# A first attention unit's queues, and the start of the second layer: who loads, subtracts and copies, and in which order

## The chip, the cores and the metric

The kernel runs on one core of one Trainium2 chip. The metric is the device time of one execution in microseconds (us), from the first to the last instruction and what lies around them. TensorE (PE) multiplies matrices, ScalarE (ACT) and VectorE (DVE) work element by element, GpSimd (POOL) does so too and issues DMAs, and SyncE (SP) issues DMAs only. Each engine has one queue, worked in order; engines wait for each other on semaphores.

## The reference

Two layers over x of shape (2, 128, 64, 64), seen as two images of 4096 positions with 128 channels.

```python
# layer 0: group norm, then attention with four heads of 32 channels
qkv = jnp.einsum('oc,bcl->bol', w_qkv, xi) + b_qkv[None, :, None]
q, k, v = jnp.split(jnp.transpose(qkv, (0, 2, 1)), 3, axis=2)
q = _apply_rotary(pos, q)          # t * cos + (t with neighbours swapped and signed) * sin
k = _apply_rotary(pos, k)
...
weight = jnp.einsum('bct,bcs->bts', qh * scale, kh * scale)
weight = jax.nn.softmax(weight.astype(jnp.float16), axis=-1).astype(weight.dtype)
a = jnp.einsum('bts,bcs->bct', weight, vh).reshape(b, c, L)
hout = jnp.einsum('oc,bcl->bol', w_proj, a) + b_proj[None, :, None]
...
# layer 1: layer norm, then attention of the tokens with themselves
scores = jnp.einsum('bsd,btd->bst', x, x)
attn_weights = jax.nn.softmax(scores, axis=-1)
return jnp.einsum('bst,btd->bsd', attn_weights, x)
...
# and then a spectral unit: causal convolutions with 16 filters by FFT, 2 x 16 matrices,
# chosen among four branches by weights from log_weights and gumbel
```

## The kernel before

**Layer 0** runs in four units: image b and pair of heads pr. A unit first prepares its operands in eight blocks of 512 positions (i, in pairs i2), and then, for each of its two heads, multiplies scores (s), takes exponentials on ACT (e, line 443) and weighs the values with them (acc). While one unit is in its scores, the next is prepared beside it. Only the first unit, `first` in the code, has nothing to hide behind: its preparation and its own first scores run together, from about 27 to 86 us.

One block of the preparation: TensorE multiplies (`first`), VectorE adds the bias and multiplies by the rotary tables `tab` (line 236, twice), adds both halves (line 240), and takes the largest value (line 243). The result t is split into two float16 terms, the first being t rounded (`hi`, on ACT in the first unit) and the second the rest t - hi (`lo`, line 242). The values are split into three bfloat16 terms: `left` is the sum with the bias (line 270), a cast makes a term (line 273), and a difference takes it off what is left (line 275), so three casts and two differences a block. In the first unit the casts are ACT's and the differences GpSimd's.

After each pair of blocks, `stacks` (lines 277 to 286) copies the terms by DMA into the stacks ks and qs, of four strips of 32 rows each: ks takes first, first, second, second; qs takes first, second, first, second. That is 16 DMAs a pair. In the first unit SyncE issues the eight of ks and four of qs, GpSimd four of qs. SyncE also issues the tables (line 224): two wait in buffers, the next is loaded when one has been used, and its place in SyncE's order is behind the stacks of the pair before.

The last step of a head is `divide`: three parts of accs are added to ao, the row of sums is brought over by DMA (rec), inverted, sent to memory and brought back (back), and multiplied in (line 355). A `wait` count says how many turns to let pass before the last product; it is 5 for the last head of layer 0, 1 for all others.

**The joint.** The second layer needs its tokens as fp32r in a first part (hi, hiT) and a second (lo, loT). The second parts were written to memory (lows) beside layer 0 and are loaded again one at a time into `low`, one buffer, and copied to loT and lo (lines 1092, 1093). Before them stands the load of fw (line 796), in space that the last unit's operands still hold. The scores of layer 1 (y, line 911) are three products of these parts; their exponentials (ey) are split again (ep, lines 968 and 969), and their transposes too (eT, lines 929 and 930).

Beside attention of the first image (`attend(0)`), a chain of steps is interleaved: the second image's layer norm, `filters` (tb, lines 812 to 818), and `matrices`. The latter begins with `branch_weights` (z, zm, soft, zs, sm, top, free, wbr; lines 830 to 851) and the 16 coef (line 872), then mu, and then makes 16 matrices pm, each a weighted sum of four (lines 726 and 728) and two differences (lines 890 and 891), from `raw` loaded two matrices ahead. The buffer of the first raw is that of mu_raw and of tb.

What sets the order: a planner places every instruction on its engine's queue by estimated times, so a change at one place can move instructions elsewhere. An instruction that is given to `tc.keep_in_program_order` comes after everything that its engine was given before it in the program; all products of `product` are pinned so. The code at the joint:

```python
fw = transform(p1)                      # line 1082
...
def ready(i):                           # called by attend(0) as block i begins
    for n in range(2) if i == 0 else [i + 1]:
        if n < NQ:
            low = p.tile([P, 2, 512], F32, tag="low", name=f"low{n}")
            nc.sync.dma_start(low, lows[n].rearrange("n p c -> p n c"))
            nc.vector.tensor_copy(loT[0][:, bass.ts(n, 512)], low[:, 0])
            nc.vector.tensor_copy(lo[0][:, bass.ts(n, 512)], low[:, 1])
```

Of the kernel before, what the change touches and what calls it, by code (L numbers as in the profile page):

```python
# [12 lines left out]
F32 = mybir.dt.float32  # L13
# [6 lines left out]
ALU = mybir.AluOpType  # L20
AX = mybir.AxisListType

P = 128
# [5 lines left out]
NQ = L // 512  # L29
# [34 lines left out]
def conv_attn_hybrid(ctx: ExitStack, tc: tile.TileContext, io):  # L64
    nc = tc.nc
# [25 lines left out]
    def pool(stack, name, bufs=1, **kw):  # L91
        return stack.enter_context(tc.tile_pool(name=name, bufs=bufs, reuse_waits="tile", **kw))
# [82 lines left out]
    def layer0(tok, px, last, side, beside_last):  # L175
# [3 lines left out]
        with ExitStack() as l0:  # L179
            p1 = pool(l0, "l0_1")  # L180
# [26 lines left out]
            def prepare(b, pr, xn):  # L207
# [9 lines left out]
                first = (b, pr) == (0, 0)  # L217
# [46 lines left out]
                def split(at, n, pv):  # L264

                    bvb = bv[:, 2 * CH * pr : 2 * CH * pr + 2 * CH].rearrange("p (g c) -> p g c", g=2)

                    pool_, tag = (p1, f"ao{at // n % 3}") if first else (p2, "left")
                    left = pool_.tile([P, n, 2, CH], F32, tag=tag, name=f"left{u}_{at}", bufs=1)
                    nc.vector.tensor_tensor(left, pv, bvb.unsqueeze(1).to_broadcast([P, n, 2, CH]), ALU.add)  # L270
                    for k in range(NV):
                        dst = v[:, at : at + n, :, CH * k : CH * k + CH]
                        (nc.scalar.copy if first else nc.vector.tensor_copy)(dst, left)
                        if k + 1 < NV:
                            (nc.gpsimd if first else nc.vector).tensor_tensor(left, left, dst, ALU.subtract)

                def stacks(i2, term):
                    for s, stack in ((1, ks), (0, qs)):
                        for g in range(2):
                            for r in range(4):  # L280
                                src = term[r // 2 if s else r % 2]
                                at = 64 * s + CH * g
                                (nc.sync if first and (s or r >= 2) else nc.gpsimd).dma_start(
                                    stack[CH * r : CH * r + CH, g, bass.ts(i2, 1024)],
                                    src[at : at + CH, :],
                                )
# [48 lines left out]
            def divide(b, h, c, accs, wait):  # L335

                u = f"{b}_{h}_{c}"
                if h == 0:  # L340
                    ao[b, c] = (last if c == 3 else p1).tile([P, 1024], F32, tag=f"ao{c}", name=f"ao{b}_{c}", bufs=1)
                own = ao[b, c][CH * h : CH * h + CH, :]
                parts = [accs[CH * n : CH * n + CH, :] for n in range(NV)]
                rec = last.tile([CH, 1024 // CH], F32, tag="rec", name=f"rec{u}")
                nc.sync.dma_start(rec, accs[NV * CH :, :].rearrange("o (r s) -> o r s", r=CH))
                nc.vector.tensor_tensor(own, parts[0], parts[1], ALU.add)
                yield
                nc.vector.tensor_tensor(own, own, parts[2], ALU.add)
                nc.vector.reciprocal(rec, rec)
                back = dram.tile([CH, 1024 // CH], F32, tag="rec", name=f"back{u}", bufs=4)  # L350
                nc.sync.dma_start(back, rec)
                nc.sync.dma_start(parts[0], back.rearrange("r s -> (r s)").partition_broadcast(CH))
                for _ in range(wait):
                    yield
                nc.vector.tensor_tensor(own, own, parts[0], ALU.mult)
                yield
# [47 lines left out]
            for n, (b, pr) in enumerate(units):  # L404
# [16 lines left out]
                for g, i, m in order:  # L421
# [20 lines left out]
                    own = slice(0, len(tiles))  # L442
# [291 lines left out]
    def layers(st, layer0):  # L734
# [10 lines left out]
        hi, lo, hiT, loT = [], [], [], []  # L745
        lows = dram.tile([NQ, 2, P, 512], F32, name="lows")
# [36 lines left out]
        left = layer0(tok, px, last, side, beside_last)  # L783
# [9 lines left out]
        def transform(p):  # L793

            fw = p.tile([P, 4, NF], F32, name="fw", bufs=1)
            nc.sync.dma_start(fw, io["fw"])
            return fw
# [24 lines left out]
        def branch_weights(p):  # L822

            lg = p.tile([P, 2, NBR], F32, name="lg")
            nc.gpsimd.dma_start(lg[:, 0, :], io["log_weights"].partition_broadcast(P))
            nc.gpsimd.dma_start(lg[:, 1, :], io["gumbel"].partition_broadcast(P))
            z = p.tile([P, NBR], F32, name="z")
            nc.vector.tensor_tensor(z, lg[:, 0, :], lg[:, 1, :], ALU.add)  # L830
            zm = p.tile([P, 1], F32, name="zm")
            nc.vector.tensor_reduce(zm, z, AX.X, ALU.max, negate=True)
            zs = p.tile([P, 1], F32, name="zs")
            soft = p.tile([P, NBR], F32, name="soft")
            nc.scalar.activation(soft, z, AF.Exp, bias=zm, accum_out=zs)
            nc.vector.reciprocal(zs, zs)
            nc.vector.tensor_scalar(soft, soft, zs, None, ALU.mult)
            sm = p.tile([P, 1], F32, name="sm")
            nc.vector.reduce_max(sm, soft, axis=AX.X)
            top = p.tile([P, NBR], F32, name="top")  # L840
            nc.vector.tensor_scalar(top, soft, sm, None, ALU.is_equal)
            free = p.tile([P, NBR], F32, name="free")
            nc.vector.memset(free, 1.0)
            for i in range(1, NBR):
                nc.vector.scalar_tensor_tensor(
                    free[:, i : i + 1], top[:, i - 1 : i], 0.0, free[:, i - 1 : i], ALU.is_equal, ALU.mult
                )
            nc.vector.tensor_tensor(top, top, free, ALU.mult)
            wbr = p.tile([P, NBR], F32, name="wbr")
            nc.vector.tensor_tensor(wbr, top, soft, ALU.subtract)  # L850
            nc.vector.tensor_tensor(wbr, wbr, soft, ALU.add)
            ends = p.tile([P, NBR, P], F32, tag="phi", name="ends")
            nc.gpsimd.dma_start(ends, io["ends"].partition_broadcast(P))
            weighted_sum(mask, ends, top)
            return wbr
# [223 lines left out]
        with ExitStack() as l1:  # L1079
            p1 = pool(l1, "l1")  # L1080
            lo.append(p1.tile([P, L], F32R, name="lo"))
            fw = transform(p1)
            with ExitStack() as part:
                p = pool(part, "l1_a")
                gate = [0]

                def ready(i):
                    for n in range(2) if i == 0 else [i + 1]:
                        if n < NQ:
                            low = p.tile([P, 2, 512], F32, tag="low", name=f"low{n}")  # L1090
                            nc.sync.dma_start(low, lows[n].rearrange("n p c -> p n c"))
                            nc.vector.tensor_copy(loT[0][:, bass.ts(n, 512)], low[:, 0])
                            nc.vector.tensor_copy(lo[0][:, bass.ts(n, 512)], low[:, 1])

                def closed(j):
                    gate[0] = j + 1

                y = [None]

                def stage(i, n):  # L1100
                    y[0] = p.tile([P, 512], F32, tag="y", name=f"y1_{i}")
                    return y[0]

                stats = LayerStats(p1, tok[1], "a1")
                steps = chain(left, stats.steps(), filters(p, fw), matrices(p), normalise(1, stats, stage, gate))
                attend(0, p1, steps, closed, ready)
            right0.close()

            mxr, mxl = (x[0].rearrange("p (k s c) -> p k s c", k=NK, s=2) for x in (hiT, loT))
            with ExitStack() as part:  # L1110
                p = pool(part, "l1_b", 2)
                fed = LayerStats(ffw, tok[1], "f1")

                def closed(j):
                    fed.take(range(4 * j, 4 * j + 4))
                    fed.close(range(4 * j, 4 * j + 4))
                    own = slice(2 * j, 2 * j + 2)
                    m = p.tile([P, 2, 2, C], F32, tag="m", name=f"m{j}")
                    nc.sync.dma_start(m, mx[own].rearrange("k p s c -> p k s c"))
                    nc.vector.tensor_copy(mxr[:, own], m)  # L1120
                    nc.vector.tensor_tensor(mxl[:, own], m, mxr[:, own], ALU.subtract)

                attend(1, p1, feed(0, p, bank, fw), closed)
# [172 lines left out]
        fw = transform(late_pool)  # L1296
# [155 lines left out]
```

## Time and profile before

| what | us |
|---|---|
| median of 3 runs | 2924.3 (2923.4 to 2927.8) |
| the profiled execution | 2924.8 |
| its span | 2923.0 |
| TensorE, VectorE, ACT, GpSimd busy | 2852.4, 1689.9, 1916.1, 653.8 |
| first exponential of the first unit | starts at 45.48 |
| last accs copy of layer 0 ends | 1028.24 |
| first use of loT by TensorE | 1033.04 |
| pm loop on VectorE | 1118.6 to 1198 |

The page gives shares over the whole span. The two places that the change touches are some 60 and some 170 us of 2923, so their waits are read from the list of waits of each engine and from the timeline. In a timeline line, the text in brackets is the idle time of the engine just before the instruction, and what ended it. SPq lines are DMA issues of SyncE: the time is that of the issue, not of the transfer. The mean granted TensorE clock of this execution was 0.993 of full speed.

### The profile page before, as it was taken

The page shows a single profiled execution, that of the slowest core. Times are in us where ns is not written, and L with a number is a line of the kernel's source. Part 1 is how long each engine was busy: PE and PEld are TensorE (multiplying, and loading weights), DVE is VectorE, ACT ScalarE, POOL GpSimd, SP SyncE. Part 2 cuts the span into 40 slices and gives each one's busy share as a digit, 9 for nine tenths or more (in the row PEclk, how much of TensorE's full clock was granted, in tenths as well). Part 3 has the DMA queues.
Part 4 walks back from the last instruction along what each step waited for, and adds up shares of the span by engine and source line. Part 5 has one row for each costly group of instructions (what it writes and reads, how often), then busy time and mean ns, then how long its engine had stood idle before and what let it go on. Part 6 is the DMA issues. An engine that isn't in the chain of part 4 may idle for free. (4 is left out here: it accounts for less than half of the span.)

```text
span 2923.0 us, 40062 instructions
## 1 busy us (share of the span) xinstructions
PE 2852.4 (98%) x13872; PEld 1815.1 (62%) x13872; DVE 1689.9 (58%) x2916; ACT 1916.1 (66%) x2507; POOL 653.8 (22%) x1312
## 2 busy tenths in 40 slices
PE   5999999999999999999999999999999999999998
PEld 3555555555455577787777885666666666666665
DVE  5265562355243289877866677555555555555554
ACT  4999999999999956565555664444444444444442
POOL 3022120022000010000102003343444444444440
PEclk9999999999999999999999999999999999999999
DMA  4122120021001024100011002333333334333331
GB/s 137 33 63 77 48 66 16 5 78 48 6 33 35 4 83 128 57 1 1 26 39 40 8 26 68 97 89 93 92 85 82 81 77 115 82 85 84 82 82 54
DMA packets 166033, 175.91 MB, mean 60 GB/s; under 512 B 45264, under 2 KB 109536, under 8 KB 165824
## 3 DMA queue, kind: packets, MB, share of 16 engines
q1 hardware_dynamic: 122528, 137.05, 16.9%
q0 software_dynamic: 40304, 32.99, 5.4%
q10 hardware_dynamic: 2992, 3.22, 0.3%
q8 instruction: 115, 1.88, 0.3%
q14 instruction: 94, 0.77, 0.1%
HBM read 130.68 MB, written 25.49 MB: 53 GB/s over the span
## 5 line engine op out<-in xcount | busy, mean ns | idle before, releaser
L443 ACT ACTIVATE e<-s 128x1536 f16<-128x1536 f32 (+1 forms) x704 | 937.4, 1427 | 34.8 <-PE s L190 29.6
L1196 DVE TENSOR_TENSOR xl<-cv,xh 128x1024 fp32r<-128x1024 f32 x512 | 603.2, 1220 | 436.3 <-ACT xh L1195 349.0
L1195 ACT CAST xh<-cv 128x1024 fp32r<-128x1024 f32 x512 | 494.6, 1018 | 522.7 <-PE cv L1186 511.8
L1161 POOL DMA_DIRECT2D tokens_in<-rows x1024 | 490.5, 487 | 680.0 <-PE cv L1186 580.7
L190 PE MATMUL s<-qs,ks 128*128 128x512 f16 x2048 | 557.7, 379 | 11.8 <-ACT e L443 7.4
L190 PE MATMUL acc<-e,v 128*97 128x512 f16 x2048 | 557.1, 379 | 3.3 <-DVE accs L391 0.2
L1218 PE MATMUL m<-xh,loT 128*128 128x512 f32 x1024 | 409.5, 400 | 0.0
L1218 PE MATMUL m<-xh,hiT 128*128 128x512 f32 x1024 | 403.0, 394 | 0.0
L190 PEld LDWEIGHTS <-v 128*97 128x97 bf16 x2048 | 254.5, 124 | 214.3 <-issue 11.8
L190 PEld LDWEIGHTS <-ks 128*128 128x128 f16 x2048 | 200.5, 99 | 232.6 <-issue 46.9
L920 ACT ACTIVATE ey<-y,nshift 128x512 f32<-128x512 f32 x288 | 195.9, 689 | 201.4 <-PE y L911 179.2
L1186 PE MATMUL cv<-tables_in,tokens_in 32*128 32x512 f32 x2048 | 300.3, 646 | 1.8 <-DVE xl L1196 1.8
L1218 PE MATMUL m<-xl,hiT 128*128 128x512 f32 x1024 | 291.8, 417 | 1.2 <-DVE xl L1196 0.5
L1218 PEld LDWEIGHTS m<-xl,hiT 128*128 128x128 f32 x1024 | 178.6, 189 | 175.7 <-issue 104.7
L1218 PEld LDWEIGHTS m<-xh,loT 128*128 128x128 f32 x1024 | 192.5, 188 | 90.7 <-issue 47.8
L1218 PEld LDWEIGHTS m<-xh,hiT 128*128 128x128 f32 x1024 | 192.3, 188 | 42.2
L930 DVE TENSOR_TENSOR eT<-eT,eT 128x512 fp32r<-128x512 f32 x224 | 147.3, 684 | 112.9 <-ACT eT L929 112.0
L937 PE MATMUL oacc<-ep,hi 128*128 128x512 f32 x576 | 209.1, 411 | 1.2 <-DVE ep L969 1.2
L969 DVE TENSOR_TENSOR ep<-ey,ep 128x512 fp32r<-128x512 f32 x288 | 191.3, 684 | 7.6 <-PE oacc L937 1.4
L391 DVE COPY accs<-acc 97x512 f32<-97x512 f32 x64 | 44.2, 691 | 253.3 <-PE acc L190 253.3
L929 ACT ACTIVATE eT<-eT 128x512 fp32r<-128x512 f32 x224 | 133.1, 605 | 55.7 <-PE eT L927 55.5
L937 PE MATMUL oacc<-eT,hi 128*128 128x512 f32 x448 | 154.1, 405 | 2.2 <-DVE oT L975 1.2
(197 smaller groups left out, 3031.3 us busy)
## 6 DMA issues: line engine op xcount, KB each, us to landing
tables_in<-tables SPq DMA_DIRECT2D x1024, 64.0 KB, 3.3
tab<-in_rot SPq DMA_DIRECT2D x32, 512.0 KB, 4.1
tokens_in<-rows POOLq DMA_DIRECT2D x1024, 16.0 KB, 3.2
rows<-uh SPq DMA_DIRECT2D x64, 128.0 KB, 1.9
qs<-term POOLq DMA_DIRECT2D x112, 64.0 KB, 2.0
ks<-term POOLq DMA_DIRECT2D x96, 64.0 KB, 1.9
accs<-back SPq DMA_DIRECT2D x32, 128.0 KB, 2.3
lows<-stage SPq DMA_DIRECT2D x16, 256.0 KB, 2.0
```

What stands on the lines that cost most here:

```text
L190: tc.keep_in_program_order(nc.tensor.matmul(*args, **kw))
L443: nc.scalar.activation(e[:, own, :], ps[:, own, :], AF.Exp, scale=SCORE_SCALE)
L920: nc.scalar.activation(e[:, 2 * h + q, :], ps[:, q, :], AF.Exp, bias=nshift, accum_out=den[:, t, i : i + 1])
L929: nc.scalar.activation(eT[0], pt, AF.Copy, accum_out=den[:, 4 * i + u, j : j + 1])
L930: nc.vector.tensor_tensor(eT[1], pt, eT[0], ALU.subtract)
L937: nc.tensor.matmul(acc, a[0][:, own], c, start=(start and t == 0 and n == 0), stop=(stop and t == len(es) - 1 and n == 2),)
L969: nc.vector.tensor_tensor(es[t][1], e[:, t, :], es[t][0], ALU.subtract)
L1161: nc.gpsimd.dma_start(ut[part, :, :], rows[b][ci, row : row + BP, w0 : w0 + WC // 2, :])
L1186: nc.tensor.matmul(pu[:, h, :], ut[grp, w % 2, :], tt[grp, w % 2, :], start=True, stop=True)
L1195: nc.scalar.copy(hi, pu.rearrange("d h (c k) -> d k h c", k=NK))
L1196: nc.vector.tensor_tensor(seconds[n % 2][:, :, w, 64 * g2 : 64 * g2 + 64].rearrange("d k (h c) -> d k h c", h=2), pu.rearrange("d h (c k) ...
L1218: nc.tensor.matmul(acc, m, x, start=(s == 0 and w == 0 and i == 0), stop=(s == 1 and w == WC - 1 and i == len(products) - 1),)
```

## The change

Four things. In the first unit the value differences go from GpSimd to VectorE. Its stacks are shared out by term: SyncE issues those of the first terms (4 of ks and 4 of qs a pair), GpSimd those of the second. In `divide`, for the last head alone, the first addition is pinned behind what VectorE was given before it. At the joint, the first low load and its copies stand ahead of fw in the program, the copy to loT is pinned, later loads come one at a time, and the first instruction of the branch weights is pinned.

```diff
                         if k + 1 < NV:
-                            (nc.gpsimd if first else nc.vector).tensor_tensor(left, left, dst, ALU.subtract)
+                            nc.vector.tensor_tensor(left, left, dst, ALU.subtract)
...
                             for r in range(4):
-                                src = term[r // 2 if s else r % 2]
+                                n = r // 2 if s else r % 2
+                                src = term[n]
                                 at = 64 * s + CH * g
-                                (nc.sync if first and (s or r >= 2) else nc.gpsimd).dma_start(
+                                (nc.sync if first and n == 0 else nc.gpsimd).dma_start(
...
-                nc.vector.tensor_tensor(own, parts[0], parts[1], ALU.add)
+                terms = nc.vector.tensor_tensor(own, parts[0], parts[1], ALU.add)
+                if wait > 1:
+                    tc.keep_in_program_order(terms)
...
-            nc.vector.tensor_tensor(z, lg[:, 0, :], lg[:, 1, :], ALU.add)
+            tc.keep_in_program_order(nc.vector.tensor_tensor(z, lg[:, 0, :], lg[:, 1, :], ALU.add))
...
-            fw = transform(p1)
             with ExitStack() as part:
                 p = pool(part, "l1_a")
                 gate = [0]
 
+                def second_parts(n):
+                    if n < NQ:
+                        low = p.tile([P, 2, 512], F32, tag="low", name=f"low{n}")
+                        nc.sync.dma_start(low, lows[n].rearrange("n p c -> p n c"))
+                        copy = nc.vector.tensor_copy(loT[0][:, bass.ts(n, 512)], low[:, 0])
+                        if n == 0:
+                            tc.keep_in_program_order(copy)
+                        nc.vector.tensor_copy(lo[0][:, bass.ts(n, 512)], low[:, 1])
+
                 def ready(i):
-                    for n in range(2) if i == 0 else [i + 1]:
-                        if n < NQ:
-                            low = p.tile([P, 2, 512], F32, tag="low", name=f"low{n}")
-                            nc.sync.dma_start(low, lows[n].rearrange("n p c -> p n c"))
-                            nc.vector.tensor_copy(loT[0][:, bass.ts(n, 512)], low[:, 0])
-                            nc.vector.tensor_copy(lo[0][:, bass.ts(n, 512)], low[:, 1])
+                    second_parts(i + 1)
+
+                second_parts(0)
+                fw = transform(p1)
```

As planned, SyncE's order at the joint becomes low 0, fw, rec, phi, low 1, back, gw, low 2, accs; before it was fw, low 0, rec, phi, gw, low 1, back, accs, low 2. On VectorE the copies of low 0 follow the last accs copy at once, two of the three ao operations come behind the copies of low 1, and the 27 instructions of branch weights and coef come behind the last tb copy. TensorE's order changes only in these 170 us.

## The prediction, made before the changed kernel was run

> **What bounds the kernel now.** I read the page first (busy times, slices), then what each engine waited for, then the timeline of two places, and last a table of busy times by stretch.
>
> ```profile
> PE 2852.4 (98%) x13872; PEld 1815.1 (62%) x13872; DVE 1689.9 (58%) x2916; ACT 1916.1 (66%) x2507; POOL 653.8 (22%) x1312
> ...
> PE   5999999999999999999999999999999999999998
> ```
>
> TensorE is busy for 98% of the span, and only its first slice is half empty. So a change pays where TensorE waits, and nowhere else. Its waits (us in total, times, longest):
>
> ```profile
> PE s L190 <- ACT e L443: 7.4, 6, 4.3
> PE y L911 <- DVE loT L1092: 5.1, 1, 5.1
> ...
> PE s L190 <- DMA qs<-term: 2.4, 1, 2.4
> ...
> PE eT L927 <- DVE loT L770: 1.7, 1, 1.7
> PE yT L766 <- DVE y L719: 1.6, 1, 1.6
> ```
>
> Lines 1 and 3 lie in the first unit, line 2 at the joint of the layers (1033 us), lines 4 and 5 at 1198 to 1202 us. The first unit in the timeline (start, length, engine):
>
> ```profile
> 28.52 0.41 DVE L270 TENSOR_TENSOR left<-first,bv 128x256 f32<-128x256 f32 x1
> 28.86 0.68 DVE L240 TENSOR_TENSOR t<-t,t 128x512 f32<-128x512 f32 x1
> ...
> 41.72 1.30 SPq L224 DMA_DIRECT2D tab<-in_rot  x2
> ...
> 44.46 0.67 POOL L275 TENSOR_TENSOR left<-left,v 128x256 f32<-128x256 f32 x1
> 45.16 0.41 ACT L273 CAST v<-left 128x256 bf16<-128x256 f32 x1 [2.83 <-POOL left L275]
> 45.48 1.44 ACT L443 ACTIVATE e<-s 128x1536 f16<-128x1536 f32 x1
> 46.51 1.41 DVE L236 SCALAR_TENSOR_TENSOR t<-first,bqk,tab 128x512 f32<-128x512 f32 x2 [3.84 <-DMA tab<-in_rot]
> 46.97 2.78 PE L190 MATMUL s<-qs,ks 128*128 128x512 f16 x6 [4.32 <-ACT e L443]
> ```
>
> The first exponential has its scores from 42.65 (the matmuls of 41.84 last 0.81), yet starts at 45.48: in ACT's queue a value cast stands before it, which waits for a difference on GpSimd, which stands behind four stack DMAs there (42.24 to 44.45). VectorE loses 3.84 us to tables that SyncE issues only after its twelve stacks. The joint:
>
> ```profile
> 1025.47 0.35 SPq L796 DMA_DIRECT2D fw<-in_fw  x1
> 1025.88 0.42 SPq L1091 DMA_DIRECT2D low<-lows  x1
> ...
> 1028.30 1.22 DVE L346 TENSOR_TENSOR ao<-accs 32x1024 f32<-32x1024 f32 x1
> ...
> 1033.04 0.79 PE L911 MATMUL y<-loT,hiT 128*128 128x512 f32 x1 [5.06 <-DVE loT L1092]
> 1033.63 0.63 PE L911 MATMUL y<-hiT,loT 128*128 128x512 f32 x1
> ```
>
> What comes after it, while the 16 pm matrices are made (columns: stretch, length, PE, PEld, DVE busy):
>
> ```profile
> 1160.00:1180.00 20.00, 20.00 (x105) 16.34 (x104) 19.77 (x47) 12.57 (x36) 0.00 (x0) 1.00 0.42 128
> ```
>
> TensorE and VectorE are both full here: VectorE can't catch up what it is late.
>
> **What the Trainium skill says.** "DMA: Bandwidth & Descriptors", section "Issuing engines are not separate DMA queues": a DMA on another queue saves only the issuing sequencer's time. I count queue time alone: a stack takes 0.62 us on SyncE (eight in 5.07 from 34.02) and about 0.5 on GpSimd; that landings stay as they were the trace of before can't show. "TensorE: Matmul & The Clock Gate", Part 1: an idle window of about 3.4 us halves the clock, and about 3.4 us of work restores it. The trace agrees: after the wait of 5.06 us, matmuls of 512 columns start every 0.43 us until 1036.6, then every 0.23. "Vector Engine (DVE) Microarchitecture Reference", section 5.2: about 1.04 ns a column and 75 ns an instruction, an estimate of 0.34 us for a 128x256 difference. The trace agrees on the neighbouring shape: L270 at 28.52 is followed by L240 at 28.86, 0.34 us later.
>
> **The change, part by part.** The forecast stands on the profiled execution, 2924.8 us; the median of the runs, 2924.3, is 0.5 below.
>
> *First unit, VectorE.* 16 differences (two for each of eight blocks) come to it at 0.34 us. A block took 3.80 (27.20 to 31.00), and takes 3.80 + 2 x 0.34 = 4.5. Four blocks from 27.20 end at 45.1 rather than 42.7. That was waiting time: block 4 started at 46.51, for its table.
>
> *First unit, queues.* Before table 4 SyncE has eight stacks rather than twelve. Their source comes about 0.7 later (34.75, VectorE being slower), so the table is issued at 34.75 + 8 x 0.63 = 39.8 instead of 41.72, and lands 4.8 later at 44.6. Block 4 starts at 45.1, 1.4 earlier, now bound by VectorE. All second-term stacks go to GpSimd: 32 instead of 16, 16 us more of issue, against 16 differences of about 0.7 (11 us) less. Per pair of blocks it issues 8 x 0.5 = 4 us in 9 us of VectorE work; nothing that TensorE waits for stands behind them.
>
> *First unit, the exponentials.* Block 3's values come at 27.2 + 3 x 4.5 + 1.3 = 42.0; three casts and two differences in turn (0.4 each with a handover) bring the first exponential to 43.9 instead of 45.48: 1.6 earlier. The bank of the next scores then waits for it as before. The planner also gives the fourth pair of scores another bank, whose reader is a VectorE addition instead of the exponential just before: about 1.0 more. From the tenth exponential on (86 us) ACT, TensorE and VectorE run in one chain, and the shift stays: **-2.6**. At 0.41 us for a difference walking the same queues gives -2.1, at 0.5 -1.3; if TensorE's wait of 4.32, shortened to about 2.4, also spares slow clock after it, -3.2 to -3.6.
>
> *Joint, the direct part.* fw lies where the last q stacks lay, and so waits for TensorE's last scores; SyncE is held by it for 21.4 us, and the low load behind it is issued at 1025.88. In front of it, low goes out near 1004 and is there long before use. The copy loT0 is pinned behind the last accs copy, which ends at 1028.24: 1028.3 instead of 1032.57. TensorE goes on at 1028.8 instead of 1033.04: 4.2. Its wait falls under 1 us, so of the ten slow matmuls (10 x 0.2 = 2 us) some are spared; but the second low (one buffer, issued after the copy of the first, near 1029.4, landing 3.6 to 5 later) holds TensorE a little near 1034. By 1048 it is 4.6 ahead.
>
> *Joint, what is late next.* The branch weights (z to coef) are 27 VectorE instructions. Ten to 1035.2 and 16 coef, at 0.14 to 0.2 us each, make 4.5 to 4.9 us. Before, they lay where VectorE had time (1031 to 1049). The pin puts them behind the last tb copy, which ended at 1101.87, with a wait for ACT's soft in their midst: zm to zs took 0.69 at 1031.5, and may take 1.3 behind two exponentials. Behind that wait stand the mask, gw, the next eT and ep rests, and mu, whose end releases the buffer of the first pm matrix. So at the pm loop VectorE has 4.6 less 4.5 less 0.8, plus what it waited there before (mu_raw 1.14, rden 0.30, raw 0.37): it starts that loop about 1 us earlier, not 4.6. In the loop it is full (19.77 of 20.00), so TensorE, 4.6 ahead, is held back, at the latest at the y and loT rests behind the loop (the waits of 1.6 and 1.7 above). Some of 1.9 us of waits for raw in the loop can vanish too. I take **-1.5** for the joint; bounds 0 (all eaten) and -4.6 (buffers cover all). After 1202 us the engines' orders are the same as before, and the rest shifts.
>
> Sum: 2924.8 - 2.6 - 1.5 = 2920.7 against the profiled run, 2920.2 against the median.
>
> **The rivals.** 0.2% is 5.8 us, about what a measurement can tell; *faster* below 2918.5, *slower* above 2930.1.
>
> A, the sum above: 2920.2, its own range 2917.5 to 2922.8. Chance 0.48.
>
> B, the joint's 4.6 arrives whole: TensorE has up to four ep and five eT rests in buffers, and the planner puts y of the first image one pm matrix earlier in VectorE's order. Against it: all VectorE work up to the last loT rest must be done in either order. 2924.3 - 2.6 - 4.6 = 2917.1. Chance 0.24.
>
> C, the first unit brings nothing, since a difference on VectorE takes what it took on GpSimd (0.66): walking on from -1.3 at 0.5 by 9 us a us gives 0. The 0.34 us spacing of L270 speaks against it. 2924.3 - 1.5 = 2922.8. Chance 0.13.
>
> D, slower: in the pm loop the attention's rests now stand up to one matrix later in VectorE's order (2.15 us of its work a matrix), and the two full engines wait for each other in turn. At x us a matrix 16 matrices cost 16x, against gains of 2.6 and 4.6: slower from x = 0.45 on. At 0.8, 2924.3 + 12.8 - 7.2 = 2929.9. For it: no slack in this stretch. Against it: before, TensorE waited only 0.5 us between 1118 and 1197. Chance 0.15.
>
> **How the numbers follow.** The predicted time is A's. Below 2918.5 lies B and a little of A: 0.32. Above 2930.1 lies the upper part of D and what I have not seen: 0.12. Between: 0.56. The range 2915.5 to 2927 holds A, B and C with their bounds and leaves out most of D.
>
> **What would show it.** In the changed profile: the second VectorE block starts near 31.7, a difference there shows 0.41; tables at 39.8, block 4 at 45.1, first exponential near 43.9, the twentieth near 83.9 (before 86.47). At the joint, TensorE's wait for loT under 1.2 us, z behind 1097, the first pm near 1118.58 - 2.6 - 1 = 1115. At 1195 to 1203, longer waits for y and loT than 1.6 and 1.7 mean A, none mean B; a pm loop longer than 80 us means D. A span moved by more than 6 us, either way, would make the sum wrong; a first exponential after 45 would break its first half.

## The result, and the profile after

The changed kernel takes 2918.0 us (median of 11 runs, 2916.6 to 2921.0) against 2924.7 for the kernel before on the same chip (11 runs): 6.7 us or 0.23% less, ratio 0.9977 with a 95% interval of 0.9970 to 0.9985. The forecast was 2920.2, or -4.1. Beside later runs it was run once more, with 0.9979 (0.9971 to 0.9987) and -6.1.

The page of the changed kernel, profiled in an execution of 2918.3 us with a span of 2916.5:

```profile
PE 2851.5 (98%) x13872; PEld 1814.7 (62%) x13872; DVE 1691.9 (58%) x2932; ACT 1914.6 (66%) x2507; POOL 647.8 (22%) x1312
```

TensorE does the same work; what is gone is mostly waiting. Its waits over the whole span (us in total, times, longest; one of 18.2 at the start, 17.7 before, is left out here as in the list of before):

```profile
...
PE s L190 <- ACT e L446: 3.8, 6, 1.7
PE oacc L940 <- DVE ep L972: 2.7, 8, 0.8
...
PE s L190 <- DVE left L270: 2.1, 2, 1.6
PE oacc L940 <- DVE ep L971: 2.1, 2, 1.1
...
PE eT L930 <- DVE loT L773: 1.7, 1, 1.7
PE y L914 <- DVE loT L1093: 1.5, 2, 0.9
```

The wait for loT at the joint fell from 5.1 to 1.5, that for the exponentials from 7.4 to 3.8, and the 2.4 for the stacks (DMA qs) is no longer in the list. The waits for the parts of ep have grown from 1.2 (L969 before) to 4.8 (L971 and L972): by 1.4 at the joint itself and by 2.2 between 1120 and 1206 us. The first unit in the timeline:

```profile
33.53 0.68 DVE L240 TENSOR_TENSOR t<-t,t 128x512 f32<-128x512 f32 x1
...
34.12 0.42 DVE L275 TENSOR_TENSOR left<-left,v 128x256 f32<-128x256 f32 x1
...
34.46 0.68 DVE L243 TENSOR_REDUCE size<-t 128x1 f32<-128x512 f32 x1
...
40.05 2.08 SPq L224 DMA_DIRECT2D tab<-in_rot  x2
...
43.30 1.44 ACT L446 ACTIVATE e<-s 128x1536 f16<-128x1536 f32 x1
...
44.25 1.41 DVE L236 SCALAR_TENSOR_TENSOR t<-first,bqk,tab 128x512 f32<-128x512 f32 x2
```

A difference takes its place for 0.34 us (34.12 to 34.46). The fifth block starts at 44.25 and waits for nothing; before, it started at 46.51 behind a table. Counted from the start of the unit, which is at 27.75 here and was at 27.20, that is 16.5 us instead of 19.3. The joint:

```profile
1020.65 0.36 SPq L799 DMA_DIRECT2D fw<-in_fw  x1
...
1023.82 0.50 PE L914 MATMUL y<-loT,hiT 128*128 128x512 f32 x1 [0.66 <-DVE loT L1093]
1024.16 0.39 PE L914 MATMUL y<-hiT,loT 128*128 128x512 f32 x1
...
1026.83 0.34 DVE L352 RECIPROCAL rec<-rec 32x32 f32<-32x32 f32 x1 [2.72 <-DMA rec<-accs]
...
1092.11 0.16 DVE L835 TENSOR_REDUCE zm<-z 128x1 f32<-128x4 f32 x1
1094.31 0.16 DVE L839 RECIPROCAL zs<-zs 128x1 f32<-128x1 f32 x1 [2.05 <-ACT soft L838]
```

TensorE waits 0.66 us rather than 5.06, and the matmuls that follow start every 0.23 us at once. VectorE has two holes that weren't there: 2.72 us for rec, where before it went on with ao, and 2.05 for soft, where before it was 0.54. Near the end of the pm loop TensorE's order is another than before, and the first two of these three waits are new (the third, 1.7, was there):

```profile
1180.84 0.50 PE L940 MATMUL oacc<-ep,hi 128*128 128x512 f32 x1 [0.99 <-DVE ep L971]
...
1184.13 0.50 PE L940 MATMUL oacc<-eT,hi 128*128 128x512 f32 x1 [0.79 <-DVE oT L978]
...
1195.70 0.88 PE L930 MATMUL eT<-ident,ey 128*128 128x128 f32 x3 [1.73 <-DVE loT L773]
```

**By stage.** I took five points that all kernels have, and compared their distances with those of the profiled execution before: the first rotary multiplication (27.20 before), the twentieth exponential (86.43), the last accs copy of layer 0 (1027.55), one matmul behind the pm loop (the 5491st of 13872, at 1207.75), and the last matmul. Stage differences in us, and on the right the mean granted TensorE clock of the same executions in three stretches (40 to 60, 1180 to 1205 and 1760 to 1800 us):

| kernel | first unit | rest of layer 0 | joint and pm loop | rest | clock at 40 | at 1180 | at 1760 |
|---|---|---|---|---|---|---|---|
| before | 0 | 0 | 0 | 0 | 0.83 | 0.93 | 0.83 |
| changed | -4.4 | -0.9 | -0.5 | -1.2 | 0.91 | 0.86 | 0.87 |
| changed, once more | -3.3 | -1.0 | +0.4 | -0.6 | 0.83 | 0.86 | 0.83 |
| first unit alone | -4.4 | -1.0 | +0.7 | -0.2 | 0.91 | 0.93 | 0.83 |
| joint alone | 0.0 | -0.2 | -2.4 | -1.2 | 0.83 | 0.93 | 0.87 |
| z not pinned | -4.4 | -0.9 | -3.1 | -1.5 | 0.91 | 1.00 | 0.87 |
| pm sums on GpSimd | -4.4 | -1.0 | +0.3 | -1.6 | 0.91 | 1.00 | 0.87 |
| stacks, no differences | -5.4 | -0.9 | -1.7 | -0.2 | 0.91 | 0.93 | 0.83 |
| differences, no stacks | +0.8 | -0.3 | -1.8 | -0.2 | 0.74 | 0.93 | 0.83 |
| z in the wait for rec | -4.0 | -1.0 | -4.6 | -0.5 | 0.91 | 1.00 | 0.83 |
| pm sums, own space | -4.4 | -0.9 | -1.8 | -0.5 | 0.91 | 1.00 | 0.83 |
| stacks by stack | -3.3 | -1.0 | -0.3 | -0.4 | 0.83 | 1.00 | 0.83 |
| stacks, z in the wait | -5.3 | -1.0 | -4.3 | -0.6 | 0.91 | 0.93 | 0.83 |
| both, pm sums own space | -4.0 | -1.0 | -2.6 | -0.3 | 0.83 | 1.00 | 0.83 |

The second and third rows are one program, and the row of the first unit alone has the joint of before: a stage of one execution is known to about 1 us. Much of that is the clock. The changed kernel's two executions agree to 0.01 us up to the third exponential (20.67 and 20.68 from the start of the unit) and are 1.20 apart at the fifth (28.35 and 29.55). The stretch around it, first of one, then of the other (the clock is the third number from the end):

```profile
40.00:60.00 20.00, 15.47 (x66) 8.05 (x66) 15.87 (x30) 13.54 (x20) 6.97 (x16) 0.91 0.70 199
40.00:60.00 20.00, 15.93 (x59) 7.97 (x60) 14.76 (x28) 13.19 (x19) 6.91 (x15) 0.83 0.65 189
```

In the first, the three score matmuls at 48.22 us take 0.81 us together; in the other the same three, at 47.88, take 1.48. At half clock, 0.91, 0.83 and 0.74 in 20 us stand for 3.6, 6.8 and 10.4 us of slow clock, steps of about 3.4. The last stage shows the same without any edit in it: the four executions with 0.87 at 1760 have -1.2 to -1.6 there, those with 0.83, as before, -0.2 to -0.6. So rows are best compared where their clocks are equal. Whether the shorter slow stretch in the first unit comes with the change or by chance, the runs don't settle: the old first unit has 0.83 in both of its executions, the stacks shared out by term have 0.91 in eight of ten.

### The profile page after: what moved, and what is told of

Read it like the earlier page. It is cut to its first block, busy times and chain, and to the rows that moved or that the text cites. A ratio compares the mean times of both kernels' runs of the same rounds, so it can differ in the third digit from the quotient of the medians.

```text
span 2916.5 us, 40052 instructions
## 1 busy us (share of the span) xinstructions
PE 2851.5 (98%) x13872; PEld 1814.7 (62%) x13872; DVE 1691.9 (58%) x2932; ACT 1914.6 (66%) x2507; POOL 647.8 (22%) x1312
## 5 line engine op out<-in xcount | busy, mean ns | idle before, releaser
L972 DVE TENSOR_TENSOR ep<-ey,ep 128x512 fp32r<-128x512 f32 x288 | 191.3, 684 | 7.0 <-ACT ep L971 1.1
```

What stands on the lines that cost most here:

```text
L972: nc.vector.tensor_tensor(es[t][1], e[:, t, :], es[t][0], ALU.subtract)
```

## The experiments

Each ran beside the kernel before on one chip. Medians of this and of before, and the ratio with its interval:

| run | this | before | difference | ratio |
|---|---|---|---|---|
| first unit alone | 2920.1 | 2925.3 | -5.2 | 0.9984 (0.9978 to 0.9991) |
| joint alone | 2922.7 | 2925.3 | -2.6 | 0.9994 (0.9986 to 1.0003) |
| z not pinned | 2918.2 | 2925.3 | -7.1 | 0.9976 (0.9966 to 0.9986) |
| pm sums on GpSimd | 2921.2 | 2925.3 | -4.1 | 0.9985 (0.9979 to 0.9992) |
| stacks, no differences | 2917.7 | 2925.3 | -7.5 | 0.9975 (0.9965 to 0.9984) |
| differences, no stacks | 2924.0 | 2925.3 | -1.3 | 0.9995 (0.9987 to 1.0003) |
| z in the wait for rec | 2915.0 | 2925.3 | -10.3 | 0.9966 (0.9952 to 0.9979) |
| pm sums, own space | 2917.1 | 2925.3 | -8.2 | 0.9972 (0.9960 to 0.9983) |
| changed, once more | 2918.9 | 2925.0 | -6.1 | 0.9979 (0.9971 to 0.9987) |
| stacks, z in the wait | 2913.9 | 2925.0 | -11.1 | 0.9962 (0.9948 to 0.9975) |
| both, pm sums own space | 2915.7 | 2925.0 | -9.3 | 0.9968 (0.9956 to 0.9980) |
| stacks by stack | 2919.9 | 2925.4 | -5.5 | 0.9982 (0.9974 to 0.9989) |

**The two halves.** The first unit alone is the kernel before with two edits:

```diff
-(nc.gpsimd if first else nc.vector).tensor_tensor(left, left, dst, ALU.subtract)
+nc.vector.tensor_tensor(left, left, dst, ALU.subtract)
...
-(nc.sync if first and (s or r >= 2) else nc.gpsimd).dma_start(
+(nc.sync if first and n == 0 else nc.gpsimd).dma_start(
```

> The kernel before with the first unit's two edits alone (differences on VectorE, stacks shared out by term). Theory: in the changed kernel TensorE's twentieth exponential is 3.9 us earlier than before, 4.3 if both are counted from the first matmul, and the rest of layer 0 adds 0.9; so the first unit alone gives -4.3 to -5.2: 2919.5 to 2920.4. Rival (the first unit is worth what I predicted, 2.6, and the further shift is chance of one execution): 2922. The joint must look as in the kernel before: TensorE waits about 5 us for loT.

The joint alone is the changed kernel with these two edits undone:

> The changed kernel with the first unit of before: the joint's edits alone. Theory (VectorE is the bound of the 173 us after the joint, and its idle time there is 12.5 us in the changed kernel against 11.8 before): TensorE gains 4.4 us at the joint, loses nearly all of it by the end of the pm loop, and the sum is -0.5 to -1.5: 2923.2 to 2924.2. Rival (the joint's gain persists): -4.4, 2920.3.

Measured: -5.2 and -2.6. The first theory's number held, -4.4 in the unit and -1.0 later in layer 0. The joint alone stands between theory and rival, and its interval takes in no change.

**Which edit of the first unit.** In the changed kernel, one edit is undone at a time. The differences back on GpSimd:

> The changed kernel with the value differences back on GpSimd: of the first unit only the sharing out of the stacks by term is left. Theory (the first exponential is early because the difference it waits for stands behind nothing on VectorE): here the third cast of block 3 waits for a difference on GpSimd behind eight stack issues of 0.5 us, so the first exponential is not earlier than 45 us and most of the first unit's gain is lost: +3 to +5 against the changed kernel. Rival (the tables' earlier issue is what counts): at most +1.5 against the changed kernel.

The stacks shared out as before:

> The changed kernel with the stacks shared out as before (SyncE twelve a pair, GpSimd four): of the first unit only the move of the differences is left. Theory: the differences alone give the first exponential its earlier start (2.6 us); the tables for block 4 come at 41.7 again instead of 40.0, and block 4 waits some 2 us on VectorE, but TensorE's scores stand before it: +0.5 to +2 against the changed kernel. Rival (the tables' earlier issue is what counts): +3 or more.

Both theories fell, and both rivals held. With the stacks alone the kernel is at -7.5, as good as the changed one; with the differences alone it has lost the first unit's gain whole. By stage, at equal clock, the differences cost 0.7 to 1.3 us: -5.4 and -5.3 without them against -4.4 and -4.0 with them (0.91), and -4.0 against -3.3 (0.83). The medians alone (-7.5 against -6.7 and -6.1) couldn't tell that. Timelines, first the stacks without the differences:

```profile
39.38 1.47 SPq L224 DMA_DIRECT2D tab<-in_rot  x2
...
42.32 1.44 ACT L446 ACTIVATE e<-s 128x1536 f16<-128x1536 f32 x1
...
45.14 0.41 DVE L270 TENSOR_TENSOR left<-first,bv 128x256 f32<-128x256 f32 x1
45.61 1.44 PE L190 MATMUL s<-qs,ks 128*128 128x512 f16 x3 [0.54 <-DVE left L270]
```

and the differences without the stacks:

```profile
42.32 1.30 SPq L224 DMA_DIRECT2D tab<-in_rot  x2
...
44.40 1.44 ACT L445 ACTIVATE e<-s 128x1536 f16<-128x1536 f32 x1
...
48.68 0.41 DVE L270 TENSOR_TENSOR left<-first,bv 128x256 f32<-128x256 f32 x1
49.15 1.44 PE L190 MATMUL s<-qs,ks 128*128 128x512 f16 x3 [1.82 <-DVE left L270]
```

The third scores need the bank that the fifth block's left (L270) empties, and that block needs its table. With the table issued at 39.4 left comes at 45.1, with the table at 42.3 at 48.7; the third exponential is at 47.27 and at 50.63. Without the stacks, the first exponential is 1.4 us earlier, against the start of the unit, for the differences' sake, and by the twentieth that is gone and 0.8 more; some of that is the clock, 0.74 here and 0.83 before (an estimate: the 1.2 us between the changed kernel's two executions is what one such step was worth). So the wait on GpSimd that I read before did not decide: here it is gone, and the gain with it. The stacks alone are no test of that wait, since with the differences back on GpSimd the planner put the first exponential in front of the cast that waits for them.

Is it the earlier table, or that first terms stand behind no second terms? A last run keeps the differences on GpSimd and gives SyncE the eight ks stacks, mixed in terms, and GpSimd the eight of qs:

```diff
-(nc.sync if first and n == 0 else nc.gpsimd).dma_start(
+(nc.sync if first and s else nc.gpsimd).dma_start(
```

> The run with the stacks shared out and the differences on GpSimd, but shared out by stack instead of by term: SyncE issues the eight of ks, GpSimd the eight of qs. SyncE has eight stacks before the next tables here too, but its first-term and second-term stacks are mixed. Theory (what counts is that tables 4 and 5 leave SyncE two us earlier, so that the fifth block's values free the bank of the third scores): as the run by term, 7 to 8 below before, third exponential 3 to 4 us earlier than before. Rival (what counts is that no first-term stack stands behind a second-term one, and no GpSimd stack ahead of its term): at most half the first unit's gain, 4 to 5 below before.

Third exponential at 47.38 (before 51.27), 2.9 earlier when counted from the unit's start (21.13 from it, against 19.77 to 20.05 in the three executions by term, and 24.08 before). The unit is at -3.3, against -4.0 by term at the same clock (last row of the table). In time -5.5, between theory and rival; not all of its distance from -7.5 is the first unit, since in this execution TensorE waits 1.5 us for ep and 1.7 for loT at the joint and comes out of it 2.2 ahead, not 4.4. The tables carry the larger part of the first unit's gain, the sorting the rest.

**The give-back after the joint.** TensorE is 4.4 us ahead behind the joint, in the changed kernel, and has lost 3.9 of it behind the pm loop, 4.5 in the other execution. In the joint alone, the stacks alone and the differences alone, where the clock at 1180 is that of before, it has lost 2.0 to 2.6. First z alone is unpinned:

```diff
-tc.keep_in_program_order(nc.vector.tensor_tensor(z, lg[:, 0, :], lg[:, 1, :], ALU.add))
+nc.vector.tensor_tensor(z, lg[:, 0, :], lg[:, 1, :], ALU.add)
```

> The changed kernel with z not pinned: the planner puts the branch weights back behind the copies of low 0, where VectorE waits 2.7 us for rec. Theory (VectorE is the bound from the joint to the end of the pm loop): the wait for rec is filled with work, the wait of 2.05 us for soft at 1094 goes, so TensorE keeps 3 to 4 us more than in the changed kernel: 2914 to 2915. Rival (the give-back comes from the order of the attention's rests among the pm matrices, not from the branch weights): no change, 2918 +- 1. A second rival: z in front holds up the first ep rests, so that the joint itself loses 1 to 2 us: 2919 to 2920.

In the stage table -3.1 rather than -0.5 and +0.4, so more is kept (at a higher clock, 1.00 against 0.86); and the second rival is there too, as loT0 now stands behind z, which waits 1.9 us for its data, and TensorE waits 2.9 for loT. By the medians (-7.1) it can't be told from the changed kernel. So z was given a third place, right behind the copies of low 0, still pinned:

```diff
+                weights = branch_weights(p)     # behind second_parts(0)
                 fw = transform(p1)
...
-        def matrices(p):
-            wbr = branch_weights(p)
+        def matrices(p, wbr, top):
```

> The changed kernel with the branch weights in a third place: called right behind the copies of low 0 (z still pinned), so that they fill VectorE's wait of 2.7 us for rec, and neither stand in front of loT0, as with z free, nor behind the last tb copy. Theory (VectorE is the bound from the joint to the end of the pm loop, and its idle time is what can be gained): the waits for rec (2.7) and soft (2.0) go, TensorE's direct gain of 4.4 us stays but for some 0.6 that the first ep rest is late: 3 to 4 us less than the changed kernel, 1 less than with z free, 2914 to 2915 where before is 2924.7. Rival (the raw transfers set the pace of the pm loop, which begins no earlier): within 1 us of the changed kernel.

Measured: -10.3. VectorE in its timeline:

```profile
1023.61 0.42 DVE L1092 CAST loT<-low 128x512 fp32r<-128x512 f32 x1
...
1024.30 0.14 DVE L833 TENSOR_TENSOR z<-lg 128x4 f32<-128x4 f32 x1
...
1027.12 0.34 DVE L352 RECIPROCAL rec<-rec 32x32 f32<-32x32 f32 x1 [2.48 <-DMA rec<-accs]
1027.38 0.09 DVE L839 RECIPROCAL zs<-zs 128x1 f32<-128x1 f32 x1
```

z and zm take 0.3 us, and ACT makes soft while VectorE waits for rec: the 2.05 us for soft at 1094 are gone, and so are the other small instructions from the stretch before the pm loop. The wait for rec itself stayed at 2.5, since its reciprocal stands next in order. The first pm matrix begins 1.7 us earlier, counted from the accs copy, than in the changed kernel. The joint's stage is -4.6, but that isn't the direct gain kept whole: the weights stand in front of the first part of ep, TensorE waits 2.1 us for it (1.1 in the changed kernel), and is 3.3 ahead behind the joint, not 4.4. It is still 3.2 ahead near the end of the pm loop, and the rest is won there, where the clock is 1.00 and was 0.93 before.

Two runs below make the cleanest pair: "stacks, no differences" and "stacks, z in the wait" differ in the place of the branch weights alone, and their clocks are equal in all three stretches. The stage is -1.7 and -4.3, the time -7.5 and -11.1 (their intervals overlap). So at equal clock the place of the weights is worth 2.6 us of the stage. With each place, though, the planner also puts the products of the pm loop in another order on TensorE, with z behind the last tb copy in the one that has the new waits at 1180 and 1184. Which of the two counts, VectorE's time or that order, no run separates.

**VectorE's load in the pm loop.** The sums of each pm matrix (32 instructions, lines 890 and 891) on GpSimd, in the changed kernel:

> The changed kernel with the sum and the difference of each pm matrix on GpSimd instead of VectorE: 32 instructions of 0.2 us off VectorE in the pm loop, 6.4 us. Theory (VectorE is the bound there): the 3.9 us that TensorE gives back between 1104 and 1190 come back, less what later raw loads cost (a buffer comes free some 0.5 us later): -3 to -4 against the changed kernel, 2914 to 2915. Rival (order, or transfers of raw, which set the pace of the loop): within 1 us of 2918.

It brought nothing: -4.1 against -6.1 and -6.7, with intervals that overlap. What VectorE waited for, between 1020 and 1206 us of that run, has in its list:

```profile
DVE pm L729 <- DMA raw<-in_mpm: 7.5, 7, 2.8
...
DVE pm L729 <- POOL raw L894: 3.0, 5, 0.8
```

10.5 us of waits, where the changed kernel has 1.9 (for raw), for 6.4 of work; the raw buffers come free later. With space of its own for the result:

```diff
-                own = raw[:, 0]
+                own = tokens_in[:, k % 2, k // 2 % 2, :2, :]
```

> The run with the sums of the pm matrices on GpSimd again, but written to space of their own (tokens_in, unused in this stage) instead of into the raw buffer, so that raw is free for the next load as soon as the weighted sum is done. Theory (with the sums on GpSimd, VectorE had 6.4 us less to do and waited 10.5 us for raw and for GpSimd instead; the raw buffers' turn is the second bound, right behind VectorE): both bounds are lower here, the waits for raw fall under 3 us, and TensorE keeps its 4 us: 3 to 4 us less than the changed kernel. Rival (pm's one buffer, which GpSimd now holds, is what VectorE waits for): no better than the changed kernel.

-8.2, 1.5 to 2.1 more than the changed kernel, with intervals that overlap: half of what the theory asked. Its pm loop takes 66.0 us from the first matrix to the last, instead of 77.8, with 7.3 us of waits for GpSimd to let go of pm. Its stage, -1.8, lies among those of the runs that leave the sums alone and have the same joint (-2.4 to +0.4), so these runs don't show that VectorE's load counts.

**The two better halves.** Stacks by term with the differences left on GpSimd, and z in the wait for rec:

> The two better halves together: stacks shared out by term with the differences left on GpSimd, and the branch weights in VectorE's wait for rec. Theory (the parts add up: the first unit is worth 5.3 without the differences on VectorE and 4.3 with them, the branch weights in the wait for rec are worth 3.5): 1 below the run with z in the wait for rec, so 10 to 12 below before. Rival (what TensorE gains in the first unit is taken at the joint, where VectorE is the bound): as that run, 10 below before. Layer 0 shifts VectorE and TensorE alike, so I hold with the theory.

and the same with the pm sums in space of their own:

> The same with the sums and differences of the pm matrices on GpSimd into space of their own (tokens_in). Theory (VectorE's load is the bound of the pm loop): 1 to 2 below the run without, 12 to 13 below before, since that move was worth 1.3 in the changed kernel with VectorE waiting 7.3 us for GpSimd to free pm. Rival (with the branch weights out of the way TensorE is no longer held back, and the wait for pm takes the place of what is won): no better than the run without.

The first is the fastest kernel measured: 2913.9 us, -11.1, 5 below the changed kernel run beside it. The stages add up, -5.3 and -4.3. The second isn't better (-9.3; its intervals overlap with the first's): its pm loop is 10 us shorter, and VectorE waits 9.1 for pm. Here its rival held. Why a pm loop that ends 10 us sooner brings nothing once the branch weights are out of the way I didn't settle; VectorE's queue is worked in order, so a wait for pm holds up the ep rests behind it as work would, but no run shows that by itself.

The changed kernel once more was for the spread:

> The changed kernel once more, on the chip of the two runs beside it, to see how far two executions of one program differ by stage. Expected: the first unit -4.3 again within 0.3 (its waits are on engines), the joint -4.4 at first and -0.5 to -2.5 at 1208 us (its waits are partly on transfers); the time 6 to 8 below before.

The joint stage, +0.4, fell outside what I gave, and the first unit, at -3.3, outside its 0.3: I had taken its waits on engines for all that can vary, and the clock does too.

## Why the prediction held, point by point

The time, 2918.0, lies in the range, but nearer to B's 2917.1 than to A's 2920.2, which was the forecast. One of the signs that I had set against the sum came true: the span moved by more than 6 us, by 6.5. The sum was 2.6 + 1.5; measured by halves it was 5.2 and 2.6, and by stage of the changed kernel 4.4 + 0.9, 0.5, and 1.2 in the rest. That the total came as near as it did is partly luck: the first unit was taken too small, and the joint, by stage of the changed kernel, too large.

*VectorE, 4.5 us a block*: 4.12 measured (27.75 to 31.87). A difference costs 0.34 as worked out, but two of them lengthened the block by 0.32, not 0.68. Before, there were three gaps for them: the maximum came 0.71 us behind the sum that it reads (28.86 to 29.57), the rest 0.65 behind the maximum, as ACT's cast of the first term ended only then (30.19; the rest starts at 30.22), and the next multiplication, which writes over what the rest reads, 0.78 behind it (30.22 to 31.00). In the changed kernel such instructions start 0.60 apart, or have a difference between them, and these 0.34 are gone. Three blocks of 0.38 less brought the first exponential 1.1 us further forward than I had it: 2.7 from the start of the unit instead of 1.6. The fifth block, put at 17.9 from the start of the unit, came at 16.5, about four times 0.38 earlier. This term of the sum was mis-sized.

*The slow clock in the first unit* was the other term: I had named it, "-3.2 to -3.6" if TensorE's shorter wait spares some, and left it out of the sum. At the clock of before the unit is -3.3, with the shorter slow stretch -4.4, so 1.2 of the 1.8 between -2.6 and -4.4 is clock. The wait of 4.32, put at 2.4, is 1.73. How much of what is left is the shorter block no run shows.

*The cause of the first exponential's lateness*, "a value cast stands before it, which waits for a difference on GpSimd": the wait was there, but moving the differences doesn't pay. Alone it makes the unit 0.8 slower, part of it clock; taken away from the changed kernel it makes it 0.7 to 1.3 faster. The step that carries the unit is the one that I gave less weight: eight stacks rather than twelve before tables 4 and 5. I had the table's time right (12.6 from the start of the unit, measured 12.3), and hung the gain on the wrong one of two waits. Three slips in the working changed nothing: 16 more stacks on GpSimd at 0.5 us are 8 us and not 16, the exponential at 86 us is the twentieth and not the tenth, and the branch weights and coef are 28 instructions and not 27.

*The rest of layer 0*, "the shift stays": another 0.9 in every kernel with the stacks shared anew, 0.2 to 0.3 in the two without. Part of it lies at one product (po) which, before, waited for ao at 467 us; the rest comes in smaller steps whose cause is open.

*The joint's direct part*, 4.2 to 4.6: 4.4 (TensorE at its 4800th matmul against the last one before the joint). Right, and the slow clock behind it was spared whole: "some" of 2 us.

*What is late next*: right in kind. TensorE's head start is given back by the end of the pm loop. Two terms were off. The wait for soft, taken at 0.8 at most, is 2.05, and the wait for rec, 2.72, I didn't count. Against that VectorE came to the pm loop 2.5 to 2.8 us earlier than before in five of the six executions that have these joint edits, z pinned behind tb and the sums on VectorE (0.7 in the stacks by stack), where I had 1. The net, -1.5, is close to the three of them that have the clock of before at 1180 (-1.7, -1.8, -2.4); the changed kernel's own two, with more slow clock there, have -0.5 and +0.4, and the stacks by stack -0.3. That the place of the branch weights gives back the gain is shown; that VectorE's load does it is not.

*Where TensorE would wait*: I named the y and loT rests behind the loop. These waits are 0.6 and 1.7, and what has grown are the waits for ep, by 3.6 us. The sign that I gave for A was wrong; its effect was not.

Rival B (all of 4.6 arrives) fits the total better than A, but by chance: the total is 6.7 with the parts of neither. C (a difference takes 0.66 on VectorE) is ruled out by 0.34. D is there in kind: in the new order TensorE waits for VectorE's ep and oT (0.99 and 0.79 near 1182). In size it isn't: the pm loop takes 77.8 us against 76.4 before, from the start of its first matrix to that of its last, about 0.1 us a matrix where D needed 0.45. In the other execution it takes 80.2, beyond the 80 that I had given as D's sign; that execution, 2919.8 us, is still faster than before.

## What to carry to other kernels

A wait that the profile names is not yet what a change is worth. Undo the edits one at a time: here one edit of two made the whole gain and the other cost 0.7 to 1.3 us, and the pair together looked as if the explanation had held. Before a stage of one execution is compared with that of another, their clocks in that stage must be equal: here one step of slow clock was worth as much as an edit. And small work that is put off lands somewhere: it goes into a hole of its engine that is there anyway (here under the wait for rec), not in front of the stretch where that engine is full.

## What I had not expected of the hardware

Two instructions of 0.34 us added to an engine that is busy for nearly all of a 3.80 us block made it only 0.32 us longer. An instruction on 128x512 that needed what the one in front wrote, or wrote over what it read, started 0.71 to 0.78 us after it, others 0.60 (29.41 to 30.01 in the changed kernel), and independent work fills the difference.

One program's stages differ by about 1 us from one execution to the next, and not evenly: with this first unit five of seven executions agree to 0.1 there (-4.4), and the one at -3.3 has about 3.4 us more of slow clock. The clock also fell where TensorE had no long pause: in the changed kernel it is 1.00 from 40 to 44 us and 0.57 from 44 to 48, around waits of 1.60 and 1.73 us with three matmuls between them.
